# The target factor of two leaky attentions, read back from a DRAM row in place of PE transposes

## The chip, the cores and the metric

The kernel runs on one core of a Trainium2 chip. What is measured is the device time of one execution in microseconds (us), from the first to the last instruction of the program. PE is TensorE (matmuls and transposes), DVE is VectorE, ACT is ScalarE, POOL is GpSimd; SP issues DMAs, as ACT and POOL can too.

## What is computed

A graph of 2708 nodes with 256 features each goes through four layers. Each is a graph operation over a dense 0/1 adjacency matrix and a feed-forward part, both with a residual:

```python
x = x + gnn(layernorm(x), adj, ...)
x = x + ffn(layernorm(x), ...)
```

The change touches the graph operations of layers 2 and 3, attentions of one and of four heads whose score is a leaky ReLU of a sum of two numbers, one of the target i and one of the source j:

```python
def _L2_gnn_ref(h, adj, W, a):
    wh = h @ W
    wh1 = wh @ a[:F_OUT, :]
    wh2 = wh @ a[F_OUT:, :]
    e = wh1 + wh2.T
    e = jnp.where(e > 0, e, ALPHA * e)
    e = jnp.where(adj > 0, e, NEG_BIG)
    attention = jax.nn.softmax(e, axis=-1)
    return jax.nn.elu(attention @ wh)

def _L3_gnn_ref(x, adj, W, a):
    h = jnp.einsum('nf,hfo->hno', x, W)
    f1 = jnp.einsum('hno,ho->hn', h, a[:, :F_out, 0])
    f2 = jnp.einsum('hno,ho->hn', h, a[:, F_out:, 0])
    e = f1[:, :, None] + f2[:, None, :]
    e = jnp.where(e >= 0, e, 0.2 * e)
    alpha = jax.nn.softmax(e + (adj == 0) * NEG_INF, axis=-1)
    return concat_heads(jnp.einsum('hij,hjo->hio', alpha, h))
```

Layer 2 has H = 1 and 256 output features, layer 3 has H = 4 and 64 a head. The exponential of the leaky ReLU is a maximum of two products, so that, with a factor of j alone taken into the values V, a weight is `max(R[i], Q[j]) * adj[j, i]`, with R a number of the target and Q one of the source. The softmax's denominator comes from a column of ones beside V.

## The kernel before

The nodes are 22 tiles of 128 (the last has 20). `GatFront` holds what an attention needs of the nodes: `V` (values and a column of ones), and `R`, `Q`, `B`, which have the node of a tile on the partitions and the tile (and head) on the columns. Its constructor loads the weights `w` and `ar` (L3422, L3425, SP's queue) and forms products of them on DVE (four multiplies L3431 into `pr`, four sums L3437). `all` or `chunk` makes V; `ready` makes R, B and Q by ACT (L3503, L3505, L3506), and POOL scales V by B tile by tile (L3511).

`fast_gat` goes over the targets in parts. In layer 2 the parts are six of 512 targets (the last of 148); in layer 3 one of 256, four of 512 and one of 404, numbered 0 to 5 here. In a part it goes over the source tiles j. For each, SP loads 128 rows of the adjacency matrix into one of eight buffers `aj` (L3579), and DVE makes for each head the weights `PT` in one instruction (L3548): the maximum of `Rr` and the column `Q[:, h, j]`, times `aj`. `Rr` is R of the part's targets along the columns, the same on all 128 partitions. PE then multiplies PT with V and adds up over j in PSUM.

In layer 2 each block of 128 targets has one matmul per source tile (L3643), with PT as the stationary operand. In layer 3 V is stationary, and a source tile has eight matmuls (L3716) whose moving operand is PT: for each head one into 64 rows of an accumulator (numerators, two heads in one accumulator) and one into 32 rows of another (denominators). The code emits the eight numerators of two source tiles, and then their eight denominators. Each of these matmuls is two instructions in the trace. The last 20 nodes as sources are taken together in one product for all heads (`last_weights`, L3588 and L3589; in layer 2 from `Rt`, which holds R of four blocks of targets on four groups of 32 partitions).

`Rr` is made by `spread`: for each head and each block of 128 targets, a PE transpose of the column of R, broadcast to 128 columns (L3558), into a PSUM tile `o_ps`, and one ACT copy per head (L3563). In layer 2 ACT also copies 32 partitions of it per block to `Rt` (L3568). `spread(0)` runs ahead of part 0 and `spread(1)` a step per source tile in it; `spread(i + 2)` runs in part i + 1, in layer 3 inside `finish`, whose steps are taken one by one between source tiles. `finish` also copies the accumulators of the part before to `oT` (L3597), transposes them (L3603), and calls what layer 3's feed-forward part does with a finished part (transposes of `fa` at L4247, gate matmuls at L4257, ranks).

The program is written in the Tile framework: buffers come from pools (a pool that is closed gives its memory to later ones, and who writes it next waits for its last readers), and a scheduler in the framework fixes the order on each engine when the program is built, by costs of its own. The order of matmuls in the trace is therefore not that of the code, and instructions can move far from their line. Each engine and each DMA queue takes its instructions in order.

Two other places come up below. In the scores of layer 2's feed-forward part PE sums over the edges (L3927, `e_ps`), DVE does a layer norm and picks the two best experts (L3935 to L3995), and PE transposes the result `top` (L4000) between matmuls of an expert (L4050, L4064). The layer-3 front is constructed before that part, and its values are made chunk by chunk in it.

Of the kernel before, what the change touches and what calls it, by code (L numbers as in the profile page):

```python
# [8 lines left out]
F32 = mybir.dt.float32  # L9
# [3392 lines left out]
class GatFront:  # L3402
# [5 lines left out]

    def __init__(self, k, W, a, H, pool, tmp):
        nc = k.nc  # L3410
# [5 lines left out]
            pool.tile([128, H, NT], F32, name=n) for n in ("R", "Q", "B")  # L3416
        )
        nc.gpsimd.memset(self.fs, 0.0)
        nc.gpsimd.memset(self.V[:, :, :, Fo : Fo + 1], 1.0)
# [73 lines left out]
    def ready(self, col):  # L3493

        k, H, fs = self.k, self.H, self.fs
        nc = k.nc
        R, Q, B = self.R, self.Q, self.B
        ex = extremes(k, fs[:, 1, :, :], H, self.tmp, "gx")
        g = ex[:, 0, :, None].to_broadcast([128, H, NT])
        rel = self.tmp.tile([128, H, NT], F32, name="rel")  # L3500
        nc.vector.tensor_tensor(R, fs[:, 0, :, :], g, ALU.add)
        nc.vector.tensor_scalar(R, R, 0.8, RANGE + 5.0, ALU.mult, ALU.min)
        nc.scalar.activation(R, R, AF.Exp)  # L3503
        nc.vector.tensor_tensor(rel, fs[:, 1, :, :], g, ALU.subtract)
        nc.scalar.activation(B, rel, AF.Exp)  # L3505
        nc.scalar.activation(Q, rel, AF.Exp, scale=-0.8)  # L3506
        spread_check(k, ex, H, col, self.tmp)
        for t in range(NT):
            p = sz(t)
            vt = self.V[:p, t, :, :]  # L3510
            nc.gpsimd.tensor_tensor(  # L3511
                vt, vt, B[:p, :, t, None].to_broadcast([p, H, D // H + 1]), ALU.mult
            )


def fast_gat(k, adjT, front, elu, parts=CHUNKS, after=None):
# [8 lines left out]
    with ExitStack() as ctx:  # L3525
        keep = ctx.enter_context(tc.tile_pool(name="g", bufs=1))
        Rr = keep.tile([128, H, N], F32, name="Rr")

# [3 lines left out]
        if H == 1:  # L3532
            Rt = keep.tile([128, len(CHUNKS), 128], F32, name="Rt")
            nc.gpsimd.memset(Rt[:, len(CHUNKS) - 1, :], 0.0)
        adjp = ctx.enter_context(tc.tile_pool(name="gadj", bufs=8))
# [14 lines left out]
        def spread(i):  # L3550

            if i >= len(parts):
                return
            c0, cs = parts[i]
            for h in range(H):
                p = psum()
                for t, o, n in blocks(c0, cs):
                    nc.tensor.transpose(  # L3558
                        p[:, o : o + n],
                        R[:n, h, t : t + 1].to_broadcast([n, 128]),  # L3560
                        k.ident[:n, :n],
                    )
                nc.scalar.copy(Rr[:, h, c0 : c0 + cs], p[:, :cs])  # L3563
                yield
            if H == 1:
                for t, o, n in blocks(c0, cs):
                    p = slice(o // 4, o // 4 + 32)
                    nc.scalar.copy(Rt[p, i, :n], Rr[p, 0, t * 128 : t * 128 + n])  # L3568
                yield

        def weights(c0, cs, j, h, aj):

            PT = ptp.tile([128, 512], F32, name="PT")
            product(PT[:, :cs], Rr[:, h, c0 : c0 + cs], Q[:, h, j : j + 1], aj[:, :cs])
            return PT
# [6 lines left out]
        def last_weights(c0, cs):  # L3582
# [3 lines left out]
            for h in range(H):  # L3586
                p = slice(32 * h, 32 * h + 32)
                nc.sync.dma_start(aj[p, :cs], adjT[N - 32 : N, c0 : c0 + cs])  # L3588
                nc.scalar.copy(Rh[p, :cs], Rr[p, h, c0 : c0 + cs])  # L3589
            product(Rh[:, :cs], Rh[:, :cs], Qt, aj[:, :cs])  # L3590
            return Rh

        def finish(c0, cs, i, acc, final):
# [4 lines left out]
            yield  # L3598
            yield from spread(i + 2)
            for t, o, n in blocks(c0, cs):  # L3600
# [26 lines left out]

        for _ in spread(0):
            pass
        side = spread(1)  # L3630
        for i, (c0, cs) in enumerate(parts):
            if H == 1:
                bl = blocks(c0, cs)
                acc = [psa.tile([128, Fo + 1], F32, name="acc_ps") for _ in bl]
                late = []
                for j in range(NT - 1):
                    PT = weights(c0, cs, j, 0, adjacency(c0, cs, j))
                    next(side, None)
                    for (t, o, n), ac in zip(bl, acc):
# [25 lines left out]
                for (t, o, n), ac in zip(bl, acc):  # L3665
# [15 lines left out]
                    )  # L3681
                side = spread(i + 2)
                continue
# [5 lines left out]
            for j0 in range(0, NT, 2):  # L3689
                nums, dens = [], []  # L3690
                for j in (j0, j0 + 1):
# [3 lines left out]
                    else:  # L3695
                        PT = last_weights(c0, cs)
                        src = [(slice(32 * h, 32 * h + 32), PT) for h in range(H)]
                    for _ in range(2 if final else 1):
                        next(side, None)
# [845 lines left out]
def model(tc, I, out):  # L4545
# [4 lines left out]
    with tc.tile_pool(name="flags", bufs=1) as fp:  # L4550
# [4 lines left out]
        with ExitStack() as ctx:  # L4555
            k = Fast(ctx, tc, I["x"], bad, adjT)
            with tc.tile_pool(name="lists", bufs=1) as lp:
# [35 lines left out]
                with ExitStack() as c2:  # L4593
                    keep = c2.enter_context(tc.tile_pool(name="g2", bufs=1))
                    with tc.tile_pool(name="g2t", bufs=1) as tmp:
                        front = GatFront(k, I["L2_gnn_W"], I["L2_gnn_a"], 1, keep, tmp)
                        front.all(tmp)
# [3 lines left out]
                right = dict(side="right")  # L4601
                keep = c3.enter_context(tc.tile_pool(name="g3", bufs=1, **right))
                c4 = ExitStack()

                def values():
# [6 lines left out]
                    made.append(  # L4612
                        GatFront(k, I["L3_gnn_W"], I["L3_gnn_a"], 4, keep, tmp)
                    )
# [84 lines left out]
```

## Time and profile before

| | us |
|---|---|
| median of 3 runs | 2408.55 |
| lowest and highest | 2408.13, 2414.51 |
| the profiled execution | 2408.92 |
| its span | 2407.1 |
| DVE's products of PT, L3548, x630 | 412.5 busy, 708 ns each |
| layer 3's attention matmuls, L3716, x2016 | 338.9 busy, 551 ns each |
| layer 2's attention matmuls, L3643, x882 | 194.7 busy, 381 ns each |
| transposes of R, L3558, x110 | 227 to 476 ns each |
| adjacency loads of 256 KB, x399 | 2.8 from issue to landing |

The times of the first three rows are of whole executions; the others are of the profiled one. Busy times of PE overlap where matmuls run in different columns of the array side by side, as the numerators of two heads do. A DMA's time runs from its issue on a queue to its landing; the queue is free for the next one after a fraction of a microsecond. In the chain of waits, each piece is work that the end of the program stood behind, in order of time. In a timeline, a bracket after a row holds the time in which its engine was idle before it, and what ended that. The mean granted clock of PE was 0.961 of full speed.

### The profile page before, as it was taken

To read this page: it belongs to the slowest core of one execution; us is meant where nothing else is said; L and a number is where in the kernel's file an instruction comes from. 1 tells how busy PE (TensorE), PEld (TensorE's weight loads), DVE (VectorE), ACT (ScalarE), POOL (GpSimd) and SP (SyncE) were. 2 spreads that over 40 slices of the span, in tenths; PEclk is the share of its full clock that TensorE was granted. 3 is DMA by queue.
4 is the path that set the end of the run, shared out by engine and by line. 5 is a ranking of instruction groups with operands and counts; after the bars stand their busy time and mean duration, and the time that the engine had idled before them with its cause. 6 is when DMAs were issued, how large, how long until landed. Compare 5 with 4: busy or idle time off the path is not lost. (4 is left out here: it accounts for less than half of the span.)

```text
span 2407.1 us, 31811 instructions
## 1 busy us (share of the span) xinstructions
PE 2263.5 (94%) x11620; PEld 1501.1 (62%) x11620; DVE 1530.9 (64%) x3386; ACT 687.1 (29%) x1388; POOL 454.6 (19%) x496
## 2 busy tenths in 40 slices
PE   7999999989899899999799999999999999969997
PEld 4777765577778676777578877666632333325664
DVE  7588888645676558456655563234499998853544
ACT  6433333213655222212230013233411112111121
POOL 1100013004100243565130002510030000002221
PEclk9999999869999999999899997999999999979998
DMA  5244322200756244332345523000033433314430
GB/s 150 66 114 115 113 79 79 72 4 12 236 176 188 62 116 96 82 77 48 78 135 150 146 67 59 21 1 18 1 85 101 117 108 110 92 55 160 130 123 15
DMA packets 158572, 219.99 MB, mean 91 GB/s; under 512 B 30911, under 2 KB 94115, under 8 KB 158404
## 3 DMA queue, kind: packets, MB, share of 16 engines
q1 hardware_dynamic: 126096, 179.84, 25.7%
q0 software_dynamic: 15488, 24.04, 4.9%
q10 hardware_dynamic: 16820, 13.95, 1.8%
q8 instruction: 95, 1.56, 0.3%
q14 instruction: 73, 0.60, 0.1%
HBM read 193.49 MB, written 24.82 MB: 91 GB/s over the span
## 5 line engine op out<-in xcount | busy, mean ns | idle before, releaser
L3548 DVE SCALAR_TENSOR_TENSOR PT<-Rr,Q,aj 128x512 f32<-128x512 f32 (+3 forms) x630 | 412.5, 708 | 95.8 <-PE acc_ps L3643 73.9
L3716 PE MATMUL acc_ps<-PT,V 128*64 128x512 f32 (+4 forms) x2016 | 338.9, 551 | 0.7 <-DVE PT L3548 0.2
L3716 PEld LDWEIGHTS acc_ps<-PT,V 128*64 128x64 f32 (+1 forms) x2016 | 95.3, 123 | 215.3 <-issue 163.1
L1844 PE MATMUL acc_ps<-fa,PT 128*128 128x257 f32 x882 | 215.4, 383 | 1.2 <-DVE out L1864 1.2
L1844 PEld LDWEIGHTS acc_ps<-fa,PT 128*128 128x128 f32 x882 | 163.9, 190 | 66.5 <-issue 33.8
L3643 PE MATMUL acc_ps<-V,PT 128*128 128x257 f32 x882 | 194.7, 381 | 1.0 <-POOL V L3511 0.9
L3643 PEld LDWEIGHTS acc_ps<-V,PT 128*128 128x128 f32 x882 | 166.1, 190 | 28.8 <-POOL V L3511 1.2
L3304 PE MATMUL h_ps<-xT,w1t 128*128 128x384 f32 x512 | 176.6, 498 | 3.7 <-ACT xT L3295 3.7
L3321 PE MATMUL y_ps<-w2t,hT 128*128 128x256 f32 x768 | 169.8, 380 | 0.0
L2511 PE MATMUL acc_ps<-V,at 128*128 128x257 bf16 x1323 | 157.1, 277 | 9.8 <-DVE at L2502 7.9
L3321 PEld LDWEIGHTS y_ps<-w2t,hT 128*128 128x128 f32 x768 | 144.9, 190 | 21.1
L2511 PEld LDWEIGHTS <-at 128*128 128x128 bf16 x1323 | 129.0, 99 | 32.9 <-DVE at L2502 5.5
L3304 PEld LDWEIGHTS h_ps<-xT,w1t 128*128 128x128 f32 x512 | 95.6, 192 | 67.9 <-ACT xT L3295 8.3
L1816 ACT ACTIVATE PT<-s_ps,rq 128x512 f32<-128x512 f32 (+1 forms) x126 | 79.5, 636 | 174.4 <-PE s_ps L1792 168.8
L3333 POOL DMA_INDIRECT acc<-ys,ids x48 | 92.0, 1916 | 154.1 <-DVE ys L3330 145.3
L4064 PE MATMUL y_ps<-w2t,hT 128*128 128x256 f32 (+1 forms) x528 | 119.9, 379 | 0.3 <-ACT hT L4057 0.3
L1792 PE MATMUL s_ps<-KT,QT 128*128 128x512 f32 (+1 forms) x252 | 116.2, 548 | 2.5 <-ACT PT L1816 1.6
L4050 PE MATMUL h_ps<-fT,w1t 128*128 128x512 f32 (+1 forms) x288 | 116.0, 552 | 1.9 <-PEq L4110 1.9
L3003 POOL DMA_INDIRECT xe<-fd,idg x48 | 79.6, 1659 | 195.1 <-DVE early_f L3034 180.8
L1817 DVE SCALAR_TENSOR_TENSOR PT<-aj,PT 128x512 f32<-128x512 int32 (+1 forms) x126 | 79.2, 633 | 57.9 <-ACT PT L1816 57.5
L4495 PE MATMUL y_ps<-w2t,hT 128*128 128x256 f32 (+1 forms) x512 | 112.8, 380 | 0.0
L4064 PEld LDWEIGHTS y_ps<-w2t,hT 128*128 128x128 f32 (+1 forms) x528 | 97.1, 186 | 21.3 <-issue 6.9
(745 smaller groups left out, 3368.8 us busy)
## 6 DMA issues: line engine op xcount, KB each, us to landing
aj<-in_adjT SPq DMA_DIRECT2D x399, 256.0 KB, 2.8
w1t<-in_L_ffn_W SPq DMA_DIRECT2D x8, 1024.0 KB
w2t<-in_L_ffn_W SPq DMA_DIRECT2D x8, 1024.0 KB
w1t<-in_L_ffn_w SPq DMA_DIRECT2D x8, 1024.0 KB, 5.6
w2t<-in_L_ffn_w SPq DMA_DIRECT2D x8, 1024.0 KB
aj<-in_adjT SPq DMA_DIRECT2D x63, 74.0 KB, 2.1
fd<-fa ACTq DMA_DIRECT2D x9, 512.0 KB, 3.1
aj<-in_adjT SPq DMA_DIRECT2D x21, 202.0 KB, 2.4
```

The source lines that it names most:

```text
L1792: nc.tensor.matmul(s[:, :cs], lhsT=QT[:, j * 128 : j * 128 + 128], rhs=KT[:, c0 : c0 + cs], start=True, stop=True,)
L1844: nc.tensor.matmul(ac, lhsT=PT[:, o : o + n], rhs=fa[:, j, :], start=j == 0, stop=False)
L2511: nc.tensor.matmul(ac[:, c:], lhsT=at[:, o : o + n], rhs=V[:, j, r], start=j == 0 and q == 0, stop=False, skip_group_check=True,)
L3304: nc.tensor.matmul(hp, lhsT=w1t[:, kk, m * 128 : (m + 1) * 128], rhs=self.xT[:, kk, :], start=(kk == 0), stop=(kk == 1),)
L3321: nc.tensor.matmul(y, lhsT=self.hT[:, m, i * 128 : (i + 1) * 128], rhs=w2t[:, m, :], start=(m == 0), stop=(m == M - 1),)
L3333: add = nc.gpsimd.indirect_dma_start(out=acc, out_offset=bass.IndirectOffsetOnAxis(ap=self.ids[:, i : i + 1], axis=0), in_=ys, in_offset=None,
L3548: nc.vector.scalar_tensor_tensor(PT, R, Q, aj, ALU.max, ALU.mult)
L3643: nc.tensor.matmul(ac[:n], lhsT=PT[:, o : o + n], rhs=V[:, j, 0, :], start=(j == 0), stop=False,)
L3716: nc.tensor.matmul(w.pop("out"), **w)
L4050: nc.tensor.matmul(o[:, :cs], lhsT=w1t[:, kk, m * 128 : (m + 1) * 128], rhs=fT[:, kk, c0 : c0 + cs], start=(kk == 0), stop=(kk == 1),)
L4064: nc.tensor.matmul(y[:n], lhsT=hT[:, m, o : o + n], rhs=w2t[:, m, :], start=(m == 0), stop=(m == M - 1),)
L4495: nc.tensor.matmul(y[:n], lhsT=hT[:, m, o : o + n], rhs=w2t[:, m, :], start=(m == 0), stop=(m == M - 1),)
```

## The change

R is transposed once as a whole (22 rows of 128 in layer 2, 88 in layer 3) by one PE transpose, copied by ACT and written to a DRAM tile `Rd` through ACT's queue. `spread(0)` makes Rr by transposes as before. For every later part, `spread` reads the part's stretch of each head's row of `Rd` with SP, broadcast to 128 partitions; it is called at the ninth source tile of the part before. Rr has 512 columns a head and two buffers in place of one buffer for all targets. In layer 2, `Rt` is read from the same row by six reads after the 13th source tile of part 0. No instruction of `finish` makes Rr any more.

```diff
-    def __init__(self, k, W, a, H, pool, tmp):
+    def __init__(self, k, W, a, H, pool, tmp, dram):
         nc = k.nc
...
         )
+        self.Rd = dram.tile([H, NT * 128], F32, name="Rd")
         nc.gpsimd.memset(self.fs, 0.0)
...
         nc.scalar.activation(Q, rel, AF.Exp, scale=-0.8)
+        n = H * NT
+        rows = self.tmp.tile([n, 128], F32, name="rows")
+        with k.tc.tile_pool(name="ps_rt", bufs=1, space=PSUM) as ps:
+            pt = ps.tile([n, 128], F32, name="rt_ps")
+            nc.tensor.transpose(pt, R.rearrange("p h t -> p (h t)"), k.ident)
+            nc.scalar.copy(rows, pt)
+        nc.scalar.dma_start(self.Rd.rearrange("h (t p) -> (h t) p", p=128), rows)
         spread_check(k, ex, H, col, self.tmp)
...
         keep = ctx.enter_context(tc.tile_pool(name="g", bufs=1))
-        Rr = keep.tile([128, H, N], F32, name="Rr")
...
         if H == 1:
-            Rt = keep.tile([128, len(CHUNKS), 128], F32, name="Rt")
-            nc.gpsimd.memset(Rt[:, len(CHUNKS) - 1, :], 0.0)
+            G = len(CHUNKS) - 1
+            Rt = keep.tile([128, G + 1, 128], F32, name="Rt")
+            nc.gpsimd.memset(Rt[:, G, :], 0.0)
+        rp = ctx.enter_context(tc.tile_pool(name="gr", bufs=2))
         adjp = ctx.enter_context(tc.tile_pool(name="gadj", bufs=8))
...
-            if i >= len(parts):
-                return
             c0, cs = parts[i]
+            Rr = rp.tile([128, H, 512], F32, name="Rr")
             for h in range(H):
+                if i:
+                    nc.sync.dma_start(
+                        Rr[:, h, :cs], front.Rd[h : h + 1, c0 : c0 + cs].to_broadcast([128, cs])
+                    )
+                    continue
                 p = psum()
...
                     )
-                nc.scalar.copy(Rr[:, h, c0 : c0 + cs], p[:, :cs])
-                yield
-            if H == 1:
-                for t, o, n in blocks(c0, cs):
-                    p = slice(o // 4, o // 4 + 32)
-                    nc.scalar.copy(Rt[p, i, :n], Rr[p, 0, t * 128 : t * 128 + n])
-                yield
+                nc.scalar.copy(Rr[:, h, :cs], p[:, :cs])
+            return Rr
+
+        def last_targets():
+            for b in range(4):
+                nc.sync.dma_start(
+                    Rt[32 * b : 32 * b + 32, :G, :],
+                    front.Rd[:, : G * 512]
+                    .rearrange("o (g b n) -> b o g n", b=4, n=128)[b]
+                    .to_broadcast([32, G, 128]),
+                )
+            for t, o, n in blocks(*CHUNKS[G]):
+                nc.sync.dma_start(
+                    Rt[o // 4 : o // 4 + 32, G, :n],
+                    front.Rd[:, t * 128 : t * 128 + n].to_broadcast([32, n]),
+                )
...
             PT = ptp.tile([128, 512], F32, name="PT")
-            product(PT[:, :cs], Rr[:, h, c0 : c0 + cs], Q[:, h, j : j + 1], aj[:, :cs])
+            product(PT[:, :cs], Rr[:, h, :cs], Q[:, h, j : j + 1], aj[:, :cs])
             return PT
...
                 nc.sync.dma_start(aj[p, :cs], adjT[N - 32 : N, c0 : c0 + cs])
-                nc.scalar.copy(Rh[p, :cs], Rr[p, h, c0 : c0 + cs])
+                nc.scalar.copy(Rh[p, :cs], Rr[p, h, :cs])
             product(Rh[:, :cs], Rh[:, :cs], Qt, aj[:, :cs])
...
             yield
-            yield from spread(i + 2)
             for t, o, n in blocks(c0, cs):
...
-        for _ in spread(0):
-            pass
-        side = spread(1)
+        nxt = spread(0)
+        side = iter(())
         for i, (c0, cs) in enumerate(parts):
+            Rr = nxt
             if H == 1:
...
                     PT = weights(c0, cs, j, 0, adjacency(c0, cs, j))
-                    next(side, None)
+                    if j == 8 and i + 1 < len(parts):
+                        nxt = spread(i + 1)
+                    if j == 12 and i == 0:
+                        last_targets()
                     for (t, o, n), ac in zip(bl, acc):
...
                     )
-                side = spread(i + 2)
                 continue
...
                         src = [(slice(32 * h, 32 * h + 32), PT) for h in range(H)]
+                    if j == 8 and not final:
+                        nxt = spread(i + 1)
                     for _ in range(2 if final else 1):
...
                     keep = c2.enter_context(tc.tile_pool(name="g2", bufs=1))
+                    dram = c2.enter_context(tc.tile_pool(name="g2d", bufs=1, space=DRAM))
                     with tc.tile_pool(name="g2t", bufs=1) as tmp:
-                        front = GatFront(k, I["L2_gnn_W"], I["L2_gnn_a"], 1, keep, tmp)
+                        front = GatFront(k, I["L2_gnn_W"], I["L2_gnn_a"], 1, keep, tmp, dram)
                         front.all(tmp)
...
                 keep = c3.enter_context(tc.tile_pool(name="g3", bufs=1, **right))
+                dram = ctx.enter_context(tc.tile_pool(name="g3d", bufs=1, space=DRAM))
                 c4 = ExitStack()
...
                     made.append(
-                        GatFront(k, I["L3_gnn_W"], I["L3_gnn_a"], 4, keep, tmp)
+                        GatFront(k, I["L3_gnn_W"], I["L3_gnn_a"], 4, keep, tmp, dram)
                     )
```

## The prediction

> **What bounds the kernel now.** I read the busy shares and the chain of waits on the page first, then the busy times stage by stage, then the chain and the timeline around the places that the change touches.
>
> ```profile
> PE 2263.5 (94%) x11620; PEld 1501.1 (62%) x11620; DVE 1530.9 (64%) x3386; ACT 687.1 (29%) x1388; POOL 454.6 (19%) x496
> ...
> PE acc_ps L3716 13%; PE y_ps L4495 4%; PE h_ps L4483 4%; PE y_ps L4064 2%; PE h_ps L4050 1%; DVE PT L3548 1%; PE v_ps L3446 1%; PE misc_ps L4257 0%; PE o_ps L3558 0%; PE o_ps L3603 0%; DMA xe<-fd,idg 0%; PE o_ps L4247 0%; DVE g L4512 0%; PE v_ps L3482 0%; PE xt_ps L4473 0%
> ```
>
> PE is busy 94% of the span, and the transposes that the change removes (L3558) stand on the chain as PE work, though with under half a per cent. By stage (columns: stretch and its length, then busy time and count of PE, PEld, DVE, ACT, POOL, then the granted clock, DMA share and GB/s):
>
> ```profile
> 1236.60:1435.00 198.40, 198.24 (x952) 167.57 (x953) 116.30 (x231) 14.89 (x41) 19.30 (x26) 1.00 0.51 143
> 1748.00:1764.12 16.12, 15.29 (x94) 7.56 (x92) 15.23 (x21) 3.67 (x8) 16.12 (x23) 0.80 0.13 34
> 1864.42:1931.36 66.94, 66.94 (x406) 21.62 (x406) 63.11 (x106) 12.40 (x32) 3.82 (x4) 1.00 0.41 115
> ```
>
> The first is the layer-2 attention, the second the beginning of part 0 of the layer-3 attention, the third its part 2. Parts 2 to 4 of layer 3 and all of layer 2 after 1236.6 leave PE no gap, so an instruction less on PE there is time gained. The beginning of part 0 is otherwise: DVE waits for little, and the chain runs over its products (L3548), while POOL scales V beside it. The chain in layer 3 (start, us, what):
>
> ```profile
> 1786.69 2.28 PE acc_ps L3716 x16
> 1788.96 0.25 PE o_ps L3558
> ...
> 1864.42 0.58 PE o_ps L3558 x4
> 1865.01 5.44 PE acc_ps L3716 x32
> 1870.44 1.02 PE o_ps L3558 x8
> 1871.46 5.44 PE acc_ps L3716 x32
> 1876.90 0.58 PE o_ps L3558 x4
> ...
> 1900.84 1.02 PE o_ps L4247 x8
> 1901.86 1.00 PE acc_ps L3716 x2
> 1902.87 1.88 PE misc_ps L4257 x16
> 1904.75 26.61 PE acc_ps L3716 x158
> ```
>
> One matmul of the program is two instructions, so x32 is a pair of source tiles j (8 numerators, 8 denominators of 512 columns), and x16 one j. Four transposes between two pairs cost 0.58 us.
>
> **Layer 3, parts 2 to 4: the gain.** Each part loses its 16 transposes: 0.58 + 1.02 + 0.58 = 2.18 us in part 2, the same in part 3, and 0.63 + 1.26 + 0.63 = 2.52 in part 4: -6.88 us. DVE doesn't take over as the bound: of the 66.94 us of part 2 it is busy 63.11, and PE will need 64.8.
>
> The order of the changed program's instructions on each engine is fixed when it is built, and gives a little of it back. Before, the transposes of R filled the time in which ACT copies the last accumulator; now each part begins with two transposes of oT, one 64-column matmul, the third transpose, then seven more matmuls. What a lone 64-column matmul costs is shown where the FFN's transposes stand now: 1.00 us for x2, and the 158 instructions that follow took 26.61; five full pairs would be 5 x 5.44 = 27.20, so 0.41 us is lost. The oT transposes in two groups (0.36 + 0.25 by the L3558 rows for two and for one) in place of one group of three (0.47) add 0.14. So 0.55 a part, for parts 2 to 4 1.65 (low bound 0, high bound 1.0 a part, the whole matmul lost). Sum for parts 2 to 4: **-5.2 us** (-6.9 to -3.9).
>
> **Layer 3, parts 0 and 1: a changed order.** Before, the scheduler issued about 12 of part 0's source tiles as pairs (8 numerators, then 8 denominators) and only some nine as "2 numerators, 1 denominator, 2 numerators, 3 denominators"; the changed program has the second form nearly throughout part 0. The second form has a row above: 2.28 us for one j at 256 columns, against 5.44 / 2 / 2 = 1.36 for a j of a pair at half the columns. The first tiles are bound by DVE, which made about five or six source tiles by 1764.1, so there the order costs nothing. From there 16 x 2.28 = 36.5 gives 1800.6, where the trace of before is done with the same tiles at 1799.08: **+1.5 us** (0, if DVE's lead decides; 2.5, if one more tile is late).
>
> Of the 0.92 us between the two forms, the rows let the denominator that stands alone take a whole slot (a sixth of a pair, 0.45 us at 256 columns), and leave 0.47 for three more changes between numerators and denominators.
>
> [...]
>
> Part 1 loses 0.47 + 0.36 + 0.58 = 1.41 us of L3558 on the chain between 1799.08 and 1864.42. It gains one split oT group, 0.55, and two pairs with a lone denominator inside. At 512 columns a slot is 5.44 / 6 = 0.91, and two more mode changes are 2/3 of 0.47 = 0.3, so 1.2 each. Sum: -1.41 + 0.55 + 2.4 = **+1.5 us** (-1.4, if the order costs nothing; +2.0). Part 5 has the order it had; it shifts.
>
> **Layer 3, start.** One transpose of R (128 columns' worth, 0.27 us as other single ones), one ACT copy of it and the issue of a DMA on ACT's queue now stand ahead of or between the first Rr copies. Before, the first transposes ran at 1747.63 and DVE's first product at 1748.89. **+0.4 us** (0.2 to 0.8).
>
> **Layer 2, start.** Of 22 transposes, 16 ran from 1232.04 beside a wait, and 6 stand in the PE-bound stretch with 1.13 us busy. Removing these: **-1.1 us**. But the first adjacency load now waits:
>
> ```profile
> 1232.04 3.69 PE L3558 MATMUL o_ps<-ident,R 128*128 128x128 f32 x16 [0.97 <-ACT R L3503]
> 1232.13 5.81 SPq L3579 DMA_DIRECT2D aj<-in_adjT  x10
> ...
> 1235.35 3.25 DVE L3548 SCALAR_TENSOR_TENSOR PT<-Rr,Q,aj 128x512 f32<-128x512 f32 x3 [3.33 <-DMA aj<-in_adjT]
> ```
>
> The adjacency buffers lie where the front's temporary pool lay. Before, the last reader there was an activation (L3506) that ended at 1232.09. Now the row tile of the new write lies there too, so SP's first load waits until the write to DRAM has landed, and every adjacency load behind it in SP's queue with it; DVE waits for that load, PE for DVE. Transpose to 1232.3, ACT copy to 1232.6, issue 1232.7, landing: writes to DRAM in this trace land in 2.0 to 3.1 us (small zero rows 2.0 to 2.9, 512 KB 3.1); I take 2.3, so the load is issued at 1235.0 in place of 1232.13: **+2.9 us** (2.6 to 3.7). Nothing covers it, as PE is full from 1236.6 on.
>
> The other reads are hidden. A part's Rr read (256 KB in layer 2, four of 256 KB in layer 3, on SP) is issued 13 or more tiles ahead of its first product: over 13 x 1.5 us in layer 2, 13 x 2.7 in layer 3. The nearest rows, broadcasts of 128 KB, land in 3.4 us. The adjacency loads that queue behind four such reads have eight buffers of lead, 8 x 2.7 = 22 us in layer 3. The Rt reads (six, after the 13th tile of part 0) are needed at tile 22. Removed ACT copies were off the path.
>
> **Layer 2 FFN: work that the scheduler moves.** Not in the diff, but in the order: the smaller Rr frees memory, the tiles lie elsewhere, and the layer-3 front's loads of w and ar and its four multiply and reduce pairs on DVE (L3431, L3437) leave their place in the layer-1 FFN (1168.03 to 1172, where PE did not wait for them) for the middle of the layer-2 scores. There the load waits for the last e_ps matmul (L3927, to 1562.3), and DVE's queue has the pairs between the steps of the layer norm that ends in top, for which PE waits:
>
> ```profile
> 1168.03 0.41 DVE L3431 TENSOR_TENSOR pr<-w,ar 128x256 f32<-128x256 f32 x1
> ...
> 1568.11 0.29 DVE L3964 RECIPROCAL mu<-mu 128x22 f32<-128x22 f32 x1 [0.87 <-ACT mu L3963]
> ...
> 1577.93 0.27 PE L4000 MATMUL top_ps<-ident,top 128*1 128x128 f32 x1 [1.01 <-DVE top L3995]
> ```
>
> w and ar are issued at 1562.4 on an idle queue and land 3.4 + 2 x 0.4 later, 1566.5; the first multiply could go at 1565.6, so it waits 0.9. Eight operations of 0.43 add 3.4, less the 0.87 in which DVE waits for ACT anyway: top comes 3.4 us later. PE has one more h_ps matmul (0.88) ahead of its wait: **+2.5 us** (1.7 if ar comes in time; 4.8 if it lands like a 1 MB load, 5.6).
>
> **Sum.** -5.2 + 1.5 + 1.5 + 0.4 - 1.1 + 2.9 + 2.5 = +2.5 us on the profiled 2408.92 us (span 2407.1 and 1.8 around it), which stands 0.4 above the median of the runs, 2408.55. So about 2411 us: 0.1% slower, inside 0.3% (7.2 us), which is about what a measurement here can tell. With all terms at one end it runs from -4.9 to +8.8 us: 2404 to 2418 is this case's own range.
>
> **Rivals.** (a) Both new waits are covered: 16%. If the row tile's write did not hold the adjacency and ar came while DVE waits for ACT, and the order cost nothing, -6.9 - 1.4 - 1.1 + 0.4 = -9.0, so 2400 us. For it: parts 2 to 4 are PE-bound without a doubt. Against: both waits stand in the changed program's order, and PE already waits 1.01 us at L4000 and 3.33 us of DVE idle stand at layer 2's start. (b) Slower by one mechanism, the weights in the layer-2 scores: 17%. If w and ar land after 1571 rather than 1566.5, all of DVE's queue stands behind them, and PE loses each us at L4000: from 4.7 us later the sum passes 7.2, at 8 us later it is 2419. For it: the load is released by PE's last e_ps, so nothing can start it sooner. Against: the DMA share between 1560 and 1580 is 0.01 and less, and the same load landed in 3.4. (c) The reads of one DRAM row are slow, and the change only swaps PE work for a DMA wait: 10%. It decides where four reads take over 22 us, 5.5 each, against 3.4 in the nearest row; 2 us late in each of five parts would give about 2421.
>
> **How the numbers follow.** Forecast, no change that can be told: 57%; (a) 16%, (b) 17%, (c) 10%. So faster 0.16, same 0.57, slower 0.27. The range for 8 in 10 takes in the forecast's own, most of (a) and the lower half of (b): 2401 to 2419.
>
> **What would show it.** Layer 2's first product of DVE near 1238.3; top_ps behind a wait of about 3.5 us; L3716 as x16 in 2.28 through part 0; parts 2 to 4 each 1.6 to 2.0 us shorter than 66.9 with PE still full. DVE idle behind a DMA of Rr, or PE gaps in parts 2 to 4, would make it wrong.

## The result, and the profile after

| | before | changed |
|---|---|---|
| median of 5 runs each, us | 2408.13 | 2422.38 |
| lowest and highest, us | 2406.68, 2414.51 | 2418.04, 2423.22 |
| span of the profiled execution, us | 2407.1 | 2421.4 |
| granted clock of PE in it | 0.961 | 0.957 |

The ratio is 1.0052 with a 95% interval of 1.0038 to 1.0066: the changed kernel is slower, by 14 us in the medians, where 2.5 us were forecast and 2419 us was the upper end of the range.

Where the time went is read from the starts of the same PE instructions in the two traces. The table gives the length of each stretch between two of them; each row begins where the one above ends. Parts are those of layer 3's attention, counted to the last matmul of each. The last columns hold a second trace of the changed kernel (e10 below) and what four more traces of the kernel before showed (e8, e9, e15, e16).

| stretch, us | before | changed | difference | changed, again | before, four more |
|---|---|---|---|---|---|
| start to the end of layer 2's front | 1230.8 | 1232.7 | +1.8 | 1227.5 | 1227.3 to 1231.8 |
| to layer 2's 7th attention matmul | 7.22 | 9.69 | +2.5 | 9.69 | 6.64 to 7.64 |
| to the last matmul of layer 2's attention | 199.79 | 199.83 | 0.0 | 201.37 | 199.80 |
| to the last e_ps of the scores | 123.93 | 123.91 | 0.0 | 125.03 | 123.2 to 123.6 |
| to top_ps | 16.17 | 17.90 | +1.7 | 17.90 | 15.67 |
| to the branch | 60.08 | 59.22 | -0.9 | 59.22 | 60.08 |
| PE waits at the branch | 1.94 | 4.88 | +2.9 | 4.63 | 2.05 to 2.36 |
| to a late chunk of layer 3's values (v_ps, 1733.91 before) | 93.95 | 95.89 | +1.9 | 96.24 | 93.95 |
| to the end of layer 3's front | 12.30 | 14.63 | +2.3 | 14.38 | 12.30, once 14.67 |
| to the first attention matmul | 3.75 | 3.61 | -0.1 | 3.61 | 3.74 to 3.85 |
| part 0 | 51.75 | 54.03 | +2.3 | 54.03 | 51.76 |
| part 1 | 62.13 | 65.09 | +3.0 | 65.10 | 62.13 |
| parts 2, 3, 4 together | 201.31 | 198.16 | -3.2 | 198.18 | 201.31 |
| part 5 and the rest, to PE's last matmul | 325.1 | 324.9 | -0.2 | 325.4 | 325.2 to 326.1 |

The differences add up to 14.1 of the spans' 14.3 us; the last 17 us of either program, behind PE's last matmul, are not in the table. The first row is the only large one ahead of the change; it moves by 4 us and more between executions of one program. The branch is the one in layer 2's FFN that skips the last expert if no node uses it (L4110, in the changed kernel L4135); it comes up in neither the diff nor the forecast.

PE is as full as it was (the page's first part):

```profile
PE 2269.7 (94%) x11524; PEld 1492.4 (62%) x11524; DVE 1527.7 (63%) x3386; ACT 668.2 (28%) x1343; POOL 453.2 (19%) x496
```

96 instructions fewer, and 6 us busier: what PE does takes longer somewhere. The start of layer 2 in the timeline of the changed kernel:

```profile
1234.48 0.31 ACTq L3514 DMA_DIRECT2D Rd<-rows  x1
1235.83 4.39 SPq L3601 DMA_DIRECT2D aj<-in_adjT  x9
...
1238.71 1.85 DVE L3557 SCALAR_TENSOR_TENSOR PT<-Rr,Q,aj 128x512 f32<-128x512 f32 x2 [4.86 <-DMA aj<-in_adjT]
```

SP's first adjacency load goes out 1.35 us after the issue of the row's write, 2.0 after R was ready (1233.82); before, 0.1 after it. DVE's idle time ahead of its first product is 4.86 us, where it was 3.33. The scores, in the timelines of SP, DVE and PE:

```profile
1566.65 0.37 SPq L3423 DMA_DIRECT2D w<-in_L_gnn_W  x1
1567.07 0.93 SPq L3426 DMA_DIRECT2D ar<-in_L_gnn_a  x2
```

```profile
1570.18 0.42 DVE L3432 TENSOR_TENSOR pr<-w,ar 128x256 f32<-128x256 f32 x1 [0.28 <-DMA ar<-in_L_gnn_a]
...
1574.29 0.42 DVE L3438 TENSOR_REDUCE w<-pr 128x4 f32<-128x256 f32 x1
1574.63 0.28 DVE L3989 RECIPROCAL mu<-mu 128x22 f32<-128x22 f32 x1
```

```profile
1583.99 0.27 PE L4025 MATMUL top_ps<-ident,top 128*1 128x128 f32 x1 [1.52 <-DVE top L4020]
```

The eight operations stand in the layer norm as the order had it, but PE waits 1.52 us and not 3.5. The branch in the timeline:

```profile
1645.08 0.19 PEld L4075 LDWEIGHTS h_ps<-fT,w1t 128*128 128x128 f32 x1 [2.36 <-ACTq L4135]
1648.09 6.47 PE L4075 MATMUL h_ps<-fT,w1t 128*128 128x512 f32 x10 [4.88 <-issue]
1648.09 0.29 PEld L4075 LDWEIGHTS h_ps<-fT,w1t 128*128 128x128 f32 x1 [2.83 <-issue]
```

PE loads one set of weights at 1645.08 and then nothing for 2.83 us, with no releaser ("issue"): it waits for nothing that a semaphore shows. Before, weights and matmuls went on at once:

```profile
1639.93 0.30 PEld L4050 LDWEIGHTS h_ps<-fT,w1t 128*128 128x128 f32 x2 [2.40 <-ACTq L4110]
1639.96 4.53 PE L4050 MATMUL h_ps<-fT,w1t 128*128 128x512 f32 x10 [1.94 <-PEq L4110]
```

Behind the stall the granted clock (the figure after PE, PEld, DVE, ACT and POOL busy) is half, and it is half again at the start of layer 3:

```profile
1648.10:1652.30 4.20, 4.20 (x6) 1.66 (x6) 0.00 (x0) 0.55 (x1) 0.00 (x0) 0.51 0.00 0
1652.30:1657.00 4.70, 4.70 (x13) 2.07 (x12) 0.00 (x0) 1.51 (x3) 0.00 (x0) 1.00 0.02 3
1740.00:1750.00 10.00, 8.05 (x36) 5.18 (x36) 5.69 (x18) 6.13 (x13) 2.95 (x15) 1.00 0.16 35
1750.00:1757.00 7.00, 4.95 (x12) 2.16 (x12) 1.71 (x11) 1.85 (x5) 0.00 (x0) 0.58 0.37 106
```

In the first trace of the kernel before, the clock is full in both places:

```profile
1640.00:1644.00 4.00, 4.00 (x10) 1.85 (x11) 0.00 (x0) 1.02 (x2) 0.00 (x0) 1.00 0.02 4
1741.00:1747.00 6.00, 3.45 (x15) 1.76 (x15) 1.96 (x10) 2.36 (x5) 0.00 (x0) 1.00 0.00 0
```

Parts 2 and 3 of layer 3 as stretches, in answer to 66.94 us and 63.11 of DVE:

```profile
1881.87:1947.92 66.05, 66.05 (x393) 20.14 (x389) 62.86 (x105) 10.30 (x28) 3.68 (x4) 1.00 0.44 126
1947.92:2013.97 66.05, 66.05 (x392) 20.13 (x388) 61.94 (x104) 10.19 (x28) 4.02 (x4) 1.00 0.43 126
```

PE is full and DVE is not, as forecast, but 0.9 us were won and not 1.6. The beginning of part 2 in PE's timeline shows why:

```profile
1881.86 0.44 PE L3624 MATMUL o_ps<-ident,oT 128*128 128x128 f32 x2
1882.23 1.07 PE L3741 MATMUL acc_ps<-PT,V 128*64 128x512 f32 x2
1883.23 0.33 PE L3624 MATMUL o_ps<-ident,oT 128*128 128x128 f32 x1
1883.49 5.50 PE L3741 MATMUL acc_ps<-PT,V 128*64 128x512 f32 x30
```

The 2.18 us of transposes are gone. But the lone 64-column matmul takes 1.00 us from start to start, and the 30 instructions that follow it 5.43, as much as the 32 of a full pair. Without the split they would be 0.47 (three transposes) and 5.44, here they are 0.37 + 1.00 + 0.26 + 5.43 = 7.06: 1.15 us more by these rows, and 1.3 by the part's length (66.94 - 2.18 = 64.76, measured 66.05).

### The profile page after: what moved, and what is told of

Its sections match the earlier page's. It is cut to its first block, busy times and chain, and to the rows that moved or that the text cites. A ratio compares the mean times of both kernels' runs of the same rounds, so it can differ in the third digit from the quotient of the medians.

```text
span 2421.4 us, 31630 instructions
## 1 busy us (share of the span) xinstructions
PE 2269.7 (94%) x11524; PEld 1492.4 (62%) x11524; DVE 1527.7 (63%) x3386; ACT 668.2 (28%) x1343; POOL 453.2 (19%) x496
## 5 line engine op out<-in xcount | busy, mean ns | idle before, releaser
L3741 PE MATMUL acc_ps<-PT,V 128*64 128x512 f32 (+4 forms) x2016 | 352.0, 553 | 0.0
```

Source lines behind the costliest of these rows:

```text
L3741: nc.tensor.matmul(w.pop("out"), **w)
```

## The experiments

In the expectations of e1 and e2, theory A is that the 14 us are the sum of the table's rows. Theory B is that the reads of the row and what they displace in the queues are the cost.

**e1 and e2, one layer at a time.** `fast_gat` of the kernel before is kept beside the new one, and one of the layers calls it with a front that writes no row:

```diff
-                    fast_gat(k, adjT, front, True)
+                    fast_gat_old(k, adjT, front, True)
```

That is e2; e1 does the same to layer 3's call.

> Layer 2 as in the changed kernel, layer 3 as before. Theory A (the 14 us are a sum: 2.5 at the start of layer 2 from the wait for the row's write, 0.9 at top_ps from the weights' products moved into the scores, 4.9 at the branch in layer 2's FFN where PE has no instructions because its code has moved by 17 instructions, 2.2 from a clock drop at the start of layer 3, 4.8 in layer 3's parts 0 and 1 from the order, -3.2 in parts 2 to 4): the start of layer 2 is 2.5 later, top_ps as before, the stall at the branch is there (PE waits 4.9 us, 1.9 before): about 2415.5 us. Theory B (the reads of the DRAM row in layer 3 and what they displace cause nearly all of it): 2410 to 2411 us, no stall at the branch.

> Layer 3 as in the changed kernel, layer 2 as before. Theory A: no wait at the start of layer 2, no stall at the branch (PE has as many instructions ahead of it as before), 0.9 at top_ps, layer 3 itself +1.8 and up to 2.2 for the clock: 2411 to 2413.5 us. Theory B: 2418 to 2420 us.

Layer 2 alone: 2419.13 us, ratio 1.0046 (1.0031 to 1.0060). Layer 3 alone: 2414.56 us, 1.0025 (1.0012 to 1.0038). Both times are higher than A had them, by 3.6 and by 1 us; B's are farther off, 8 us too low and 3.4 too high at the least. The stretches decide: with layer 2 alone its start takes 9.71 us and PE waits 5.23 at the branch, with layer 3 as in the kernel before to 0.01 us a part. With layer 3 alone the start of layer 2 takes 7.62, the branch 2.32, top_ps is late as in the changed kernel (17.90), and the parts have the changed kernel's lengths. So the stall at the branch comes with the edit of layer 2, and the weights' move with that of layer 3.

**e3, the code's place.** Transposes that nothing uses, after `spread(0)` of layer 2:

```diff
         nxt = spread(0)
+        if H == 1:
+            p = psum()
+            for t in range(17):
+                nc.tensor.transpose(
+                    p[:, t % 4 * 128 : t % 4 * 128 + 128],
+                    R[:, 0, t : t + 1].to_broadcast([128, 128]),
+                    k.ident,
+                )
+            dead = tmp.tile([128, 512], F32, name="dead")
+            nc.scalar.copy(dead, p)
```

> The changed kernel with 17 transposes of R added on PE at the start of layer 2, where PE waits for the first adjacency load; nothing uses them. PE has as many instructions ahead of the branch as before. Theory A (the stall at the branch is one of fetching PE's instructions and depends on where they lie): the stall falls from 4.9 to about 1.9 us, and the matmuls behind it run at full clock: 2417 to 2418 us. Rival (the stall comes from another engine that reaches the branch late, or from the loads that moved): it stays at 4.9, 2422 us or more.

2415.43 us, ratio 1.0029 (1.0018 to 1.0040), 7 us below the changed kernel in the medians, where A had 4 to 5; PE waits 2.07 us at the branch. It is more PE work and less time. The traces show 2.8 us of the gain at the branch itself; the matmuls behind it ran at half clock here too (95.65 us to the late chunk), so that part of theory A did not come out.

**e4, the row tile's place in layer 3.**

```diff
-        rows = self.tmp.tile([n, 128], F32, name="rows")
+        rows = self.pr.rearrange("p h f -> p (h f)")[:n, :128]
```

> The changed kernel with the row tile put into the buffer pr of the front, which is free by then, so that the front's pool has the size it had before. The loads of w and ar and DVE's four pairs are back in the layer-1 FFN. Theory A: top_ps waits 1.0 us again in place of 1.5, and the PE delay there, 0.9 us, goes; the start of layer 2 and the branch are as in the changed kernel: 2421.5 us. Theory C (the moved work is worth more than that, since it also shifts the clock drop at the start of layer 3): 2419 us.

2419.86 us (1.0044, 1.0030 to 1.0058). From the last e_ps to top_ps 15.67 us, as in the traces of before, and the weights' products are back in layer 1's FFN. So 512 bytes a partition in the front's pool moved the loads and eight DVE operations by 400 us of the program. Rr is as small here as in the changed kernel; the forecast's reason, the smaller Rr, was wrong. The total can't decide between A's 2421.5 and C's 2419, since executions spread by 8 us (2413.57 to 2421.68); the start of layer 3 still had a half-clock stretch (13.87), which speaks against C.

**e5, the order at the start of a part.** One more step in `finish`:

```diff
                 nc.scalar.copy(o_[:, :cs], ac[:, :cs])
             yield
+            yield
             for t, o, n in blocks(c0, cs):
```

> The changed kernel with one more step between the copies to oT and their transposes, so that these stand between two pairs and no 64-column matmul stands alone among them. Theory (the lone matmul and the split group cost 1.29 us in each of parts 1 to 4, where 0.55 was forecast): a part 2 to 4 takes 64.8 us in place of 66.05, part 1 1.3 less: -5.2 us on the changed kernel's 2422.4, about 2417. Rival (DVE is the bound of these parts, and PE waits instead): a part stays above 65.7 us, with idle time of PE before L3741 and DVE as its releaser; 2420 us or more.

2412.41 us (1.0012, 0.9995 to 1.0029), 10 us below the changed kernel, where 5 were expected. PE's timeline of part 3:

```profile
1944.57 5.51 PE L3742 MATMUL acc_ps<-PT,V 128*64 128x512 f32 x32
1950.01 0.88 PE L3625 MATMUL o_ps<-ident,oT 128*128 128x128 f32 x6
1950.82 5.51 PE L3742 MATMUL acc_ps<-PT,V 128*64 128x512 f32 x32
1956.26 0.87 PE L3625 MATMUL o_ps<-ident,oT 128*128 128x128 f32 x6
1957.06 10.95 PE L3742 MATMUL acc_ps<-PT,V 128*64 128x512 f32 x64
1967.94 1.09 PE L4273 MATMUL o_ps<-ident,fa 128*128 128x128 f32 x8
1968.96 5.51 PE L3742 MATMUL acc_ps<-PT,V 128*64 128x512 f32 x32
1974.40 1.95 PE L4283 MATMUL misc_ps<-wg,fT 128*128 128x8 f32 x16
1976.28 29.13 PE L3742 MATMUL acc_ps<-PT,V 128*64 128x512 f32 x168
2005.34 1.09 PE L3742 MATMUL acc_ps<-PT,Vt 32*64 32x512 f32 x8
...
2008.34 5.51 PE L3742 MATMUL acc_ps<-PT,V 128*64 128x512 f32 x32
```

In parts 2 to 4 no pair is cut any more, also not around the FFN's transposes of fa, where the kernel before cut one too. The parts 1 to 5 take 63.64, 64.73, 63.77, 63.77 and 67.91 us, against 65.09, 66.05, 66.06, 66.06 and 69.09 in the changed kernel: 8.5 us in all. The rival is out: parts 3 and 4 both take 63.77 us with PE full, though DVE is busy 63.16 us in the one and 60.12 in the other.

**e6 and e7, layer 3 mended.** e6 has layer 2 of the kernel before, the row in pr and the later transposes. e7 makes the second part's Rr by transposes too, a head at a time while part 0 runs:

```diff
-                if i:
+                if i > 1:
...
+        late = row()
+        side = spread(1, late)
```

> Layer 3 as in the changed kernel with the row in pr and the later oT transposes, layer 2 as before. Theory A: no wait at the start of layer 2, none at the branch above that of before, top_ps 0.5 earlier; part 0 +2.3, part 1 +1.7, parts 2 to 4 -6.6 together: -3.1, about 2405 us. Theory B (reads of the row hold layer 3): 2414 us as in the run with layer 3 alone.

> As the run before, but parts 0 and 1 get their Rr by transposes, the second while part 0 runs, as in the kernel before; reads from part 2 on. Theory A (part 0 is slower in the changed kernel because, without the transposes between them, the matmuls of a source tile are ordered with lone denominators): part 0 ends within 1 us of before, against +2.3: -5 to -7 us on before, 2401 to 2404 us. Rival (part 0 is later because of DVE or POOL at the start of layer 3): part 0 still ends 2 us later, 2405 us.

e6: 2402.23 us, ratio 0.9981 (0.9966 to 0.9996). e7: 2398.90 us, ratio 0.9959 (0.9943 to 0.9974), the lowest median here and, by its interval, faster than the kernel before. Part 0 takes 54.03 us in e6, as in the changed kernel, and 51.12 in e7, against 51.75 before. The products are the same in both. e7 also drops the four reads of part 1 from part 0, but no read held PE there: in the changed kernel it was busy in all of the 35.88 us from 1764.12 to 1800.00. So part 0's loss is the order of its matmuls, more of which the transposes between them had kept in pairs. How the scheduler comes to it stays open. Both medians lie below their expectations, which were written before e5 had run and counted 5 us for it where it gave 8.5; layer 3's six parts alone are 6.4 us (e6) and 9.4 us (e7) shorter than before.

**e8 to e10, the same programs again.**

> The kernel before once more, for its trace: which pieces differ between two executions of the same program. Theory (the half-clock stretches behind the branch and at the start of layer 3, 1.5 to 2.2 us each, come and go between executions of one program): some of them show here, or the stage ahead of layer 2, which the change does not touch, differs by up to 4 us. Rival (they belong to the changed program): neither shows, all stages within 0.5 us of the first trace.

> The kernel before a third time, for its trace. If the half-clock stretch at the start of layer 3 (seen in six of the seven changed kernels that have a trace, in neither of two traces of before) comes by chance with a share of about 0.8, it should show here; if it belongs to the programs, neither it nor one behind the branch shows, and the time from the branch to the start of layer 3 is that of the first trace within 0.3 us.

> The changed kernel a second time, for its trace. Theory: what belongs to the program repeats within 0.3 us (start of layer 2 +2.5, top_ps +0.9, the stall at the branch 4.9, parts 0 to 4 of layer 3 +2.1 in sum); the stage ahead of layer 2 differs by up to 4 us, and the half-clock stretches behind the branch (1.9) and at the start of layer 3 (2.2) may or may not repeat.

The table has the results (2407.70, 2406.54 and 2420.82 us, one execution each). All that was put down to the programs repeats, within 0.4 us but for layer 2's long stretch (201.37) and the one behind it (125.03). The first row does not: the changed kernel had 1232.7 and 1227.5, so its +1.8 is no effect of the change. e8 and e9 showed no half clock behind the branch or in layer 3's front.

**e11 and e12, layer 2.** e11 gives the row tile a buffer of its own; e12 has that and all the other mends, both layers by reads.

```diff
+        self.rows = pool.tile([H * NT, 128], F32, name="rows")
...
-        rows = self.tmp.tile([n, 128], F32, name="rows")
+        rows = self.rows
```

> The changed kernel with the row tile in a buffer of its own, so that the first adjacency load of layer 2 doesn't wait until the row's write has landed. Theory: layer 2's first product is 2.5 us earlier than in the changed kernel, that is where it stands in before (within 0.5 us, counted from the end of the front); everything else as in the changed kernel, the stall at the branch too. Rival (the transposes' place, not the wait, makes it late): it stays 2 us or more later.

> Both layers read the row from DRAM, with what was found taken out: the row in a buffer of its own in layer 2 and in pr in layer 3, the later oT transposes, layer 3's parts 0 and 1 by transposes, and 17 transposes at the start of layer 2 so that PE's code lies as before. Theory: layer 2's own gain is at most the few transposes in its full stretch, 0.3 to 1.1 us, so the time is that of the kernel with layer 2 as before or 1 us less: 2397.5 to 2399.5 us. Rival (layer 2's reads cost something besides the wait at the start): 2401 us or more.

The start of layer 2 in e11's timeline:

```profile
1228.30 4.44 SPq L3602 DMA_DIRECT2D aj<-in_adjT  x9
...
1228.92 0.31 ACTq L3515 DMA_DIRECT2D Rd<-rows  x1
1231.01 2.18 DVE L3558 SCALAR_TENSOR_TENSOR PT<-Rr,Q,aj 128x512 f32<-128x512 f32 x2 [2.82 <-DMA aj<-in_adjT]
```

The loads go out ahead of the write, and the 7th matmul comes 7.98 us after the front, against 9.69: the wait was worth 1.7 us here, and not 2.5 (2418.17 us, one execution). In e12 it comes after 6.65; in kernels with the old layer 2 after 6.64 to 7.97, so this stretch itself varies by 1.3. The clock does it: the first matmul comes 5.28 us after the front in e11 and 5.27 in e12, and from there to the 7th it takes 2.70 us at a clock of 0.50 in e11 and in the changed kernel, 1.38 at 1.00 in e12 and before. e12: 2399.97 us (0.9957, 0.9942 to 0.9971), 0.5 us above its expectation, with e7's ratio to the kernel before (0.9959): the reads of layer 2 neither gain nor cost anything that can be told.

**e13 to e16, the stall and the clock.** e3 with 64 and with 128 transposes, and the kernel before twice.

> The changed kernel with 64 transposes of R at the start of layer 2 that nothing uses (128 instructions of PE more ahead of the branch; some of them come after the first adjacency load has landed, so layer 2 starts some 2 us later). Theory: the instruction loads of 16 KB in the trace hold 256 instructions, and PE stalls where the branch leads to the end of one; with 128 instructions more it leads to the middle: PE waits 1.9 to 2.4 us at the branch. Rival (the stall comes with the change, and 17 transposes took it away by chance): it is 4.6 to 5.3.

> The same with 128 transposes, 256 instructions of PE, one whole load of 16 KB more than the changed kernel; layer 2 starts some 10 us later. Theory: the branch again leads to the end of a load: the stall is back, 4.6 to 5.3 us, with one weight load of PE ahead of it. Rival (more instructions ahead of the branch take the stall away, wherever they end): 1.9 to 2.4 us.

> The kernel before a fourth time, for its trace. Half-clock stretch at the start of layer 3 (0 of 3 traces of before, 10 of 11 of changed kernels): if it comes by chance with the same share in all programs, it should be here with 0.8; if it belongs to the programs, not.

> The kernel before a fifth time, as the run before. Without the half-clock stretch in both, a common share of 0.8 is excluded for practical purposes, and it counts as following from the programs, by a way that stays open.

The branch in e13's timeline, then in e14's:

```profile
1640.17 0.50 PEld L4085 LDWEIGHTS h_ps<-fT,w1t 128*128 128x128 f32 x2 [2.67 <-ACTq L4145]
1640.20 8.75 PE L4085 MATMUL h_ps<-fT,w1t 128*128 128x512 f32 x16 [2.20 <-PEq L4145]
```

```profile
1646.83 0.19 PEld L4085 LDWEIGHTS h_ps<-fT,w1t 128*128 128x128 f32 x1 [2.36 <-ACTq L4145]
1649.58 9.52 PE L4085 MATMUL h_ps<-fT,w1t 128*128 128x512 f32 x16 [4.62 <-issue]
```

With half a load more no stall, with a whole one the stall is back, with the one weight load ahead of it (one execution each: 2413.53 and 2424.94 us, and 2404.87 and 2411.98 for e15 and e16). e16 shows the half-clock stretch at the start of layer 3 (14.67 us, clock 0.50 from 1742 to 1749), e13 of the changed kind does not (12.30), and neither does e2.

## Why the prediction was wrong

**The step that failed: the sum had no term for the branch.** Between top_ps and the start of layer 3 the forecast added nothing and gave no reason: it went by the order of the instructions on every engine, and in the order the branch is the same. What changed is where PE's code lies: 17 instructions of the program fewer ahead of the branch, two PE instructions each. Six of six traces with that code have a wait of 4.63 to 5.23 us there, eleven of eleven with 17 or 64 more 1.90 to 2.36 (five of them of the kernel before), and the one with 128 more has 4.62. Both traces show 95 loads of 16384 bytes on the instruction queue q8. Between two of them lies a median of 254.5 of PE's matmuls and weight loads in the trace of before, and of 255 in that of the changed kernel. These lines give the rate from 1640 to 1650 us in slices of 0.25 us, the changed kernel's first and then that of before:

```profile
GB/s 0 0 0 0 0 0 0 0 0 66 0 0 0 0 0 0 0 0 0 0 0 0 66 0 0 0 0 0 0 0 0 0 0 0 0 0 0 0 0 0
GB/s 0 66 0 0 0 0 0 0 0 0 0 0 0 0 0 0 0 0 0 0 0 0 0 0 0 0 0 0 0 0 0 0 0 0 0 0 0 0 0 0
```

In the changed kernel one load starts at 1642.4 and one at 1645.5, 0.4 us after PE's single weight load, and PE goes on at 1648.1; before, they started at 1637.2 and 1640.4, the second again 0.4 us after PE's first weight load, and PE worked on through it. By these times the branch leads to the last instructions of one load, and the next is fetched only then. This is the author's reading of the loads' times and of the position (17 more, in e3), since no trace shows which instructions a load holds. The period rests on one trace each of e13 and e14: 128 transposes, 256 instructions of PE, bring the stall back, and 64 do not. By the waits of all 18 traces, 4.62 to 5.23 us against 1.90 to 2.36, the stall cost 2.3 to 3.3 us here.

**The half clock behind it, +1.9 us, and at the start of layer 3, +2.3.** The half clock behind the branch follows the stall in all seven traces that have one (93.95 us becomes 95.7 to 96.7). Without the stall it is absent in five traces of the kernel before and in e6 and e7, and there with 1.6 to 1.7 us in e2, e3, e12 and e13. When it comes can be read from the traces' record of the clock. In each of the 18 traces, all changes of the clock stand whole multiples of 3.413 us apart (to 0.001 us in the first traces of the two kernels), on a grid that lies differently in each. In the changed kernel's trace the clock is half from 1645.36, full from 1652.18 and half from 1751.17: 2 and 29 steps. PE waits at the branch and again, for 2.2 us, at the start of layer 3: 36 waits in the 18 traces. The clock was half behind every wait of which 2.06 us or more fell into one step of the grid (2.73 at the branch and 2.22 at layer 3's start in the changed kernel's first trace), and behind none with 1.88 or less (1.68 and 1.88 in the first trace of before); of the two between (1.93 and 1.96) it was half behind the first alone. A wait of 4.6 us puts 2.3 or more into one step wherever it lies, and the half clock came behind all seven stalls; behind a wait of 2 us it came only where the grid fell so. This is what the waits at these two places show, and no rule for others: at 1450.55 in the trace of before the clock also halves, with PE busy on matmuls of 24 columns.

The wait of 2.2 us at the start of layer 3 stands in every trace. The half clock there follows all seven stalls, and comes in five of the eleven traces without a stall, one of them of the kernel before. Behind a half clock at the branch the full clock returns on the grid, and the work from there to the wait takes nearly the same time, so that the wait meets the grid in nearly the same place: in all eleven such traces it ends between 0.9 us ahead of a grid point and 0.4 behind one, and in the nine of them that have both half clocks it is 98.99 us, 29 steps, from the full clock's return to the second. By these figures the 2.3 us, too, came with the stall here, though they can come without it. Together the branch and the clock are 7.1 of the 14.3 us; without them the median would be about 2415 us by this estimate, inside the range, and e3, with 17 transposes more, has 2415.43.

**Parts 2 to 4: mechanism right, size wrong.** The gain was put at -5.2 us and measured -3.2. The term for the split pair was 0.55 us a part and is 1.3 (parts 2 and 3; 1.15 in part 4). It was priced by the row around the FFN's transposes, where the 158 instructions behind the lone matmul took 26.61 us, less than five pairs of 5.44, so that it seemed to be half made good. But the last of these pairs, the one with the last 20 nodes, is shorter. In e5's lines its last 24 instructions take 3.00 us (2005.34 to 2008.34), and the 168 ahead of them 29.06, which is five pairs and 1.86 for its first eight: 4.86 in all. Four pairs and this one make 26.62, so the lone matmul's 1.00 us was lost whole there too, and nothing is made good behind the oT transposes either. The high bound of 1.0 was too low as well. e5 confirms it: it takes both cuts away, and parts 3 and 4 are 2.29 us shorter, 1.3 for the one and 1.0 for the other.

**Part 1: +1.5 forecast, +3.0 measured,** by the same term: 1.41 us of transposes gone, 1.3 for the split pair, which leaves 3.1 for the two pairs with a lone denominator, in place of 2.4. If the 0.92 us between the two forms followed the number of changes alone, the two places would have cost 2 x 2/3 x 0.92 = 1.2, so the slots weigh more. No run shows the 0.3 us that the sum has for two "mode changes"; the runs show only the two pairs as a whole, 3.1 us.

**Part 0 and the start of layer 3: +1.9 forecast, +2.1 measured** (54.03 - 51.75 - 0.14). e7 shows the order as its cause.

**The start of layer 2: +1.8 forecast (2.9 - 1.1), +2.5 measured.** The wait was forecast with 2.9 us and is 1.7 by e11: the row's write was given 2.3 us to land, and SP's load goes out 1.35 us after its issue. The half clock between the first and the 7th matmul is 1.3 of the +2.5, and had no term. The gain of 1.1 is not there: four of the six transposes stood together at 1349.15 in the trace of before and took 0.48 us, but without them the 16 matmuls behind took 4.09 us in place of 3.63, and from one part of layer 2 to the next it is 37.66 us with these four and 37.63 without. A busy PE in the trace is not a PE that sets the pace to the last tenth.

**The scores: +2.5 forecast, +0.9 measured,** 1.4 against the other traces of before. top_ps comes 1.7 to 2.2 us later, not 3.4: ar landed in 3.0 us and DVE waited 0.28 for it, not 0.9, and small operations filled gaps that ACT had left. The reason was wrong (e4): not Rr's size but the row tile in the front's pool.

**What held.** No read of the row held anything that set the pace. The two reads of 256 KB whose landing the changed kernel's trace shows took 4.0 and 5.0 us, one in e12 5.9, beyond the nearest rows' 3.4; they are hidden by lead. DVE once sat idle 1.38 us behind such a read (at 1376.8, in layer 2), which the forecast had named as a sign of being wrong; PE did not wait for it. DVE did not become the bound. Of the rivals, (a) fell, (b) fell with ar landing in 3.0 us, (c) fell by e1, e2 and e12.

The forecast's terms for layers 2 and 3 sum to +2.5 us and measure +5.3 (2.5 + 0.9 + 2.1 + 3.0 - 3.2); the branch with the half clock behind it adds 4.9, and the half clock at layer 3's start 2.3. The remaining 1.8 us of the profile's 14 belong to the stage ahead.

## What to carry to other kernels

Price the order that the scheduler makes, and not the instructions that an edit removes: here transposes of 2.2 us a part had kept matmuls in pairs, and a step later in a generator was worth more than taking them away. A small tile in a reused pool is an edit too; see who loads into that memory next. If a branch stands behind an edit, look at PE's wait there: here it was 4.88 us in place of 1.94 though the branch was not edited. A few harmless instructions ahead of it settle the question (2.07 us with 17 transposes, in e3), and without that a difference of a few us between two kernels says little about the edit.

## What was not expected of the hardware

At one branch PE waited 4.62 to 5.23 us in seven traces and 1.90 to 2.36 in the other eleven, and what set them apart was the number of PE's instructions ahead of it (e3, e13, e14). Each of the seven was followed by 3.8 to 5.7 us at half clock, 4.1 in the changed kernel's first trace. In the 18 traces the clock changed only on a grid of 3.413 us, and at the two places above it was half behind a wait with some 2 us or more in one of its steps. In the changed kernel's part 2 a lone 64-column matmul of 512 columns cost 1.00 us, a little more than a slot with two side by side (0.91, a sixth of a pair's 5.44 us), and the matmul that lost its partner was not paired again. 17 transposes that nobody needs took the stall away (4.88 to 2.07 us), and the median of the changed kernel was 7 us lower with them.
